# Two-layer attention hybrid on one core: three recurrence chains with two chunk lengths, a step-paired layout, zero products, and the last 128 queries on their own

## The chip, the cores and the metric

One core of a Trainium2 chip runs the whole program. The metric is the device time of one execution in microseconds (us), as the median of several runs. Before the change: 2581.43 us, median of 3 runs (2579.11 to 2581.67).

## What is computed

The input x is 4 batches of 128 channels by 4096 positions, fp32. Layer 0 normalizes by groups of channels and adds full attention over the positions (queries and keys of 64 channels, softmax over 4096 keys). Layer 1 normalizes over channels (written `_ln_t`) and adds causal attention with 128 channels. Then comes the part that this change is mostly about:

```python
def _L1_ffn_ref(x, W, V, gamma, beta):
    Wx = jnp.einsum('bti,hi->bth', x, W)
    flat = Wx.reshape(B * T, H)
    mean = jnp.mean(flat, axis=0); var = jnp.var(flat, axis=0)
    Wx = ((flat - mean) * jax.lax.rsqrt(var + BN_EPS) * gamma + beta).reshape(B, T, H)
    def step(yt, wx_t):
        yt = jax.nn.sigmoid(wx_t + yt @ V.T)
        return (yt, yt)
    _, ys = jax.lax.scan(step, jnp.zeros((B, H)), jnp.swapaxes(Wx, 0, 1))
    return jnp.swapaxes(ys, 0, 1)
...
x = x + _L0_conv_ref(_gn(x), ...)
t = _to_tokens(x)
t = t + _L1_attn_ref(_ln_t(t), ...)
t = t + _L1_ffn_ref(_ln_t(t), ...)
```

The mean and variance run over all 4 x 4096 tokens, so no step of the recurrence can start before the last query of the last batch is through the attention.

## The kernel before

**Attention.** For each batch, layer 0 and then layer 1 are cut into tiles of 512 queries (QT). A tile walks over its keys in units of two blocks of 128 keys. `score` issues the products of a unit (L892 for layer 1, L899 for layer 0) into a PSUM pair and ScalarE's exp (L901, L905); on the diagonal GpSimd zeroes the upper triangle of a block (L908). `product`, one unit behind, adds the exponentials into a running sum on VectorE (L933, `total`) and multiplies them with the values (L936, `av`). After a tile, `finish` folds `total` over the keys' partitions (L766 to L781: an add, a transpose, a reduction, small copies, a reciprocal, a transpose back), scales (L783, `o`), projects (L795, `po`) and adds the residual (L798). `ffn` then takes the layer norm of that tile (L689 transposes, L693 and L695 statistics, L561 and L562 the reciprocal root, the last on GpSimd), spreads it (L705 to L709), multiplies by W (L748, `pw`), scales (L752), copies the result into the recurrence's store WX (L753) and takes batch statistics (L758). These pieces are generators: `step` advances them once per unit, so they run between the units of the next tile. `following` and LAST = 3 give an order to the tiles of the last batch's layer 1: tile 3 comes last, in two halves of 256 queries.

**Recurrence.** The 4096 steps of a batch are cut into 128 chunks of 32 that run side by side as columns. Each chunk but the first starts from 0.5 and warms up over the last 12 steps of the chunk before it (WARM), so there are 12 + 32 = 44 steps. Two chains run in turn: batches 0 and 1, and batches 2 and 3, each with 2 x 128 = 256 columns. A step of a chain (`advance`) is one fp32 product with V (L1024, two TensorE instructions) onto a PSUM tile that already holds the scaled input, and one sigmoid (L1025) that writes into WX in place. `seed` puts the scaled input of four steps into PSUM (L1014, VectorE); a product with zeros first (L1008, `nil`) marks a new PSUM tile as written. WX is laid out as [batch, step in chunk, chunk], so one step's 256 columns are contiguous. Before the chains, the batch statistics are folded (L985), and the gain takes a reciprocal root on GpSimd (L561, L562, L988).

**Result.** X holds t in order of position, so step l of all chunks is every 32nd element. `residual` adds WX to it (L1029): for batches 0, 1 and most of 2 on GpSimd during the chains, for the rest of 2 and all of 3 on VectorE after them. Then all four batches are stored in halves of 1 MB from SP's and ScalarE's queues (L1053). Meanwhile the chunks' warm-up values are compared with the true ones (L1061 to L1074, `ok`, `wrong`); every engine loads the verdict (L1082) and branches (L1083) past a general version of the kernel, which isn't run here. Order within an engine is that of the built program: a scheduling layer may move an instruction ahead of others that it doesn't depend on.

Of the kernel before, what the change touches and what calls it, by code (L numbers as in the profile page):

```python
# [464 lines left out]
CHUNK = 32  # L465
# [5 lines left out]
BL = 4  # L471
LAST = 3
# [3 lines left out]
def fast_kernel(  # L476
# [14 lines left out]
    NP = N // (2 * P)  # L491
    NC = N // CHUNK
    G = 4
    assert C == P and 2 * CQ == P and N % QT == 0 and NC == P
# [60 lines left out]

    WXp = [wxpool.tile([P, 2, CHUNK, NC], F32, name=f"WX{g}") for g in range(B // 2)]
    WX = [WXp[b // 2][:, b % 2] for b in range(B)]
# [6 lines left out]
    with ExitStack() as actx:  # L564
# [71 lines left out]
        def keys0(b, c):  # L636

            if c == 0:
                K0[b] = kv.tile([P, N], F32R, tag="K0", name=f"K0_{b}")
                QR[b] = kv.tile([P, N // 2], F32, tag="QR", name=f"QR_{b}")  # L640
                V0[b] = WX[B - 1].rearrange("p l s -> p (l s)").rearrange("p (n c) -> p n c", c=C)
# [95 lines left out]
        def ffn(b, c, off, w):  # L737
            name = f"f_{b}_{c}_{off}"
            cols = ds(c * QT + off, w)
            src = X2[b][:, cols]  # L740
            if b < len(kept):
                nc.sync.dma_start(out=kept[b][:, cols], in_=src)
            yield
            _, _, rstd = deviations(src, 1e-5, name)
            yield
            rb = spread(rstd, name)
            pw = misc(f"pw_{name}")[:, :w]
            nc.tensor.matmul(pw, lhsT=FWc, rhs=src, start=True, stop=True)  # L748
            if off == 0:
                wt[b, c] = tmp.tile([P, QT], F32, tag="w", name=f"w_{name}")  # L750
            part = wt[b, c][:, ds(off, w)]
            nc.vector.tensor_tensor(part, pw, rb, ALU.mult)  # L752
            nc.scalar.copy(  # L753
                WX[b][:, :, ds((c * QT + off) // CHUNK, w // CHUNK)].rearrange("p l s -> p s l"),
                part.rearrange("p (s l) -> p s l", l=CHUNK),
            )
            if off + w == QT:
                nc.vector.bn_stats(stats_f[:, b * NQ + c, :], wt.pop((b, c)))  # L758
            yield

        def finish(b, layer, c, off, w, av, total):

            name = f"{layer}_{b}_{c}_{off}"
            k = w // 32
            t = tmp.tile([P, QT], F32, tag="a", name=f"t_{name}")[:, :w]
# [19 lines left out]
            )  # L785
            cols = ds(c * QT + off, w)
# [5 lines left out]
            yield  # L792
            yield
            po = misc(f"po_{name}")[:, :w]
# [8 lines left out]
        units, following = [], {}  # L803
        for b in range(B):
            for layer in range(2):
                order = list(range(NQ))
                if (b, layer) == (B - 1, 1):
                    order.append(order.pop(LAST))
                following.update({(b, layer, c): d for c, d in zip(order, order[1:])})
                for c in order:  # L810
                    halves = [(0, QT // 2), (QT // 2, QT // 2)] if (b, layer, c) == (B - 1, 1, order[-1]) else [(0, QT)]
                    for off, w in halves:
                        n = (c * QT + off + w) // (2 * P) if layer else NP
                        units += [(b, layer, c, off, w, u, n) for u in range(n)]
# [22 lines left out]
        def begin_tile(b, layer, c):  # L837
# [19 lines left out]
            else:  # L857
# [5 lines left out]
                if (b, 1, c) in following:  # L863
                    d = following[b, 1, c]
                    todo.insert(0, ("q1", b, d))
                    made["q1", b, d] = after(b, d)
# [9 lines left out]
        def score(i):  # L876
# [11 lines left out]
            first = [max(j0 + h, 0) * P if layer else 0 for h in range(2)]  # L888
            for h in range(2):
                lhsT = (X if layer else K0)[b][:, ts(2 * u + h, P)]  # L890
                if layer:
                    nc.tensor.matmul(  # L892
                        ps[:, h, first[h] : w], lhsT=lhsT, rhs=q[:, off + first[h] : off + w],
                        start=True, stop=True,
                    )
                    continue

                for k in range(2):
                    nc.tensor.matmul(ps[:, h, :], lhsT=lhsT, rhs=q[:, k, :], start=k == 0, stop=k == 1)  # L899
            if not layer:  # L900
                nc.scalar.activation(s, ps, AF.Exp, bias=shift)  # L901
            for h in range(2 if layer else 0):
# [3 lines left out]
                if j0 >= 0:  # L906
# [7 lines left out]
        def product(i):  # L914
# [7 lines left out]
            both = first[0] == first[1]  # L922
            if u == 0:
                if not both:
                    nc.vector.memset(total[:, 1, : first[1]], 0.0)
                for h in (slice(0, 2),) if both else range(2):
                    f = 0 if both else first[h]
                    nc.vector.tensor_copy(total[:, h, f:w], s[:, h, f:w])
            else:
                for h in (slice(0, 2),) if both else range(2):  # L930
                    f = 0 if both else first[h]
# [3 lines left out]
            for h in range(2):  # L935
                nc.tensor.matmul(  # L936
                    av[:, first[h] : w], lhsT=V[:, 2 * u + h, :], rhs=s[:, h, first[h] : w],
                    start=u == 0 and h == 0, stop=u == n - 1 and h == 1,
# [6 lines left out]
            if u == n - 1:  # L945
# [28 lines left out]
    with ExitStack() as fctx:  # L974
# [20 lines left out]
        nil = small.tile([P, QT], F32R, name="nil")  # L995
        nc.vector.memset(nil.bitcast(F32), 0.0)
        first = [small.tile([P, 2, NC], F32, name=f"first{g}") for g in range(B // 2)]
        for g in range(B // 2):
            nc.vector.memset(first[g], 0.5)
        steps = list(range(CHUNK - WARM, CHUNK)) + list(range(CHUNK))  # L1000
        nk = len(steps) // BL
        where = {}

        def seed(g, k):
            ps = where[g, k] = ps_y.tile([P, BL, 2, NC], F32, tag=f"y{g}", name=f"py{g}_{k}")
            if k < 2:
                for j in range(0, BL, 2):
                    nc.tensor.matmul(  # L1008
                        ps[:, j : j + 2].rearrange("p j h s -> p (j h s)"), lhsT=nil[:, :P], rhs=nil,
                        start=True, stop=True,  # L1010
                    )
            j0, lo = steps[k * BL], int(k * BL < WARM)
            for js in [slice(j, j + 1) for j in range(BL)] if k == 0 else [slice(0, BL)]:
                nc.vector.tensor_scalar(  # L1014
                    ps[:, js, :, lo:].rearrange("p j h s -> p h j s"),
                    WXp[g][:, :, j0 + js.start : j0 + js.stop, : NC - lo], gain, None, ALU.mult,
                )

        def advance(g, k, j):
            n, lo = k * BL + j, int(k * BL < WARM)  # L1020
            dst = first[g][:, :, 1:] if lo else WXp[g][:, :, steps[n], :]
            y = dst if lo else first[g] if n == WARM else WXp[g][:, :, steps[n] - 1, :]
            ps = where[g, k][:, j, :, lo:]
            nc.tensor.matmul(ps, lhsT=FV, rhs=y, start=False, stop=True, skip_group_check=True)  # L1024
            nc.scalar.activation(dst, ps, AF.Sigmoid, bias=bias)  # L1025

        def residual(eng, b, ls, cols=slice(0, NC)):
            xj = X[b].rearrange("p (s l) -> p l s", l=CHUNK)[:, ls, cols]
            eng.tensor_tensor(xj, xj, WX[b][:, ls, cols], ALU.add)  # L1029

        for k in range(2):
            for g in range(B // 2):
                seed(g, k)
        for k in range(nk):
            for j in range(BL):
                for g in range(B // 2):
                    advance(g, k, j)
            if k == WARM // BL - 1:
                for g in range(B // 2):
                    nc.vector.memset(first[g][:, :, 0:1], 0.0)  # L1040
            for g in range(B // 2 if k + 2 < nk else 0):
                seed(g, k + 2)
            if k * BL >= WARM:
                ls = slice(steps[k * BL], steps[k * BL] + BL)
                for b in range(3 if k < nk - 2 else 2):
                    residual(nc.gpsimd, b, ls)
        residual(nc.vector, 2, slice(CHUNK - 2 * BL, CHUNK))
        for h in range(2):
            residual(nc.vector, 3, slice(0, CHUNK), ts(h, NC // 2))
        for b in range(B):  # L1050
            for h in range(2):
                cols = ts(h, N // 2)
                (nc.scalar if h else nc.sync).dma_start(out=out[b, :, cols], in_=X[b][:, cols])  # L1053


        ones = small.tile([P, P], F32, name="ones")
        nc.vector.memset(ones, 1.0)
        ok = small.tile([P, B, NC], F32, name="ok")
        nc.vector.memset(ok, 0.0)
        for b in range(B):  # L1060
            nc.vector.tensor_tensor(  # L1061
                ok[:, b, 1:], first[b // 2][:, b % 2, 1:], WX[b][:, CHUNK - 1, : NC - 1], ALU.subtract
# [4 lines left out]
        nc.vector.tensor_reduce(good[:, 0:1], ok.rearrange("p b s -> p (b s)"), AX.X, ALU.min)  # L1067
# [3 lines left out]
        pf = ps_y.tile([P, BL, 2, NC], F32, tag="y0", name="pflag")[:, 0, 0, :]  # L1071
# [52 lines left out]
```

## Time and profile before

| | us |
|---|---|
| median of 3 runs | 2581.43 |
| the profiled execution, whole | 2581.84 |
| its span, first to last instruction | 2580.0 |
| TensorE busy in the span | 2510.6 (97%) |
| VectorE busy | 1761.0 (68%) |
| ScalarE busy | 1140.3 (44%) |
| GpSimd busy | 227.7 (9%) |
| end of the last attention product | 2476.2 |
| first product of the recurrence | 2495.74 |
| end of the last sigmoid | 2553.70 |
| first issue of a store, last one | 2554.80, 2565.95 |

All times in the text are counted from the span's start. A group of instructions stands as: line, engine, operation, out<-in with shapes, count, then busy time and mean duration of one in ns, then the idle time of its engine just before and what ended it. In a table of stretches (windows) each engine has its busy time and the count, and PEclk is the share of full TensorE clock that was granted. A matmul's duration contains some 0.16 us in which the next one already runs, so products are counted here by the distance between starts.

### The profile page before, as it was taken

To read this page: it belongs to the slowest core of one execution; us is meant where nothing else is said; L and a number is where in the kernel's file an instruction comes from. 1 tells how busy PE (TensorE), PEld (TensorE's weight loads), DVE (VectorE), ACT (ScalarE), POOL (GpSimd) and SP (SyncE) were. 2 spreads that over 40 slices of the span, in tenths; PEclk is the share of its full clock that TensorE was granted. 3 is DMA by queue.
4 is the path that set the end of the run, shared out by engine and by line. 5 is a ranking of instruction groups with operands and counts; after the bars stand their busy time and mean duration, and the time that the engine had idled before them with its cause. 6 is when DMAs were issued, how large, how long until landed. Compare 5 with 4: busy or idle time off the path is not lost.

```text
span 2580.0 us, 21857 instructions
## 1 busy us (share of the span) xinstructions
PE 2510.6 (97%) x7436; PEld 1350.5 (52%) x7436; DVE 1761.0 (68%) x3513; ACT 1140.3 (44%) x1386; POOL 227.7 (9%) x297
## 2 busy tenths in 40 slices
PE   7999999999999999999999999999999999999975
PEld 4555554444555555444555555444455555544552
DVE  6776667567867677666777666755786766776564
ACT  4444444444444444444444444444444444344444
POOL 2010001101000100010100010110100000000005
PEclk9999999999999999999999999999999999999988
DMA  2000000000100000000100000000010000000013
GB/s 73 1 0 1 0 1 13 9 4 5 37 1 1 1 0 5 13 5 9 37 1 0 1 0 1 13 9 4 5 37 1 1 1 1 1 0 1 1 66 132
DMA packets 11944, 31.30 MB, mean 12 GB/s; under 512 B 2096, under 2 KB 2864, under 8 KB 10032
## 3 DMA queue, kind: packets, MB, share of 16 engines
q1 hardware_dynamic: 8928, 24.12, 2.6%
q10 hardware_dynamic: 2896, 5.71, 0.6%
q8 instruction: 60, 0.98, 0.2%
q14 instruction: 60, 0.49, 0.1%
HBM read 15.14 MB, written 14.68 MB: 12 GB/s over the span
## 4 chain that ended last, share of the span: by engine, by line
PE 88%; DVE 8%; issue 2%; POOL 1%; ACT 1%; POOLq 0%; DVEq 0%; ACTq 0%
PE av L936 47%; PE ps L899 17%; PE ps L892 16%; PE py L1024 2%; DVE total L933 2%; PE po L795 1%; PE pv L666 1%; PE pk L650 1%; PE pq L731 1%; PE pw_f L748 1%; POOL rstd_f L562 1%; PE pt L689 1%; DVE lst_f L693 0%; DVE t L766 0%; ACT s L901 0%
## 5 line engine op out<-in xcount | busy, mean ns | idle before, releaser
L933 DVE TENSOR_TENSOR total<-total,s 128x1024 f32<-128x1024 f32 (+4 forms) x802 | 881.2, 1102 | 569.0 <-ACT s L901 325.6
L936 PE MATMUL av<-s,WX 128*128 128x512 f32 x2048 | 964.9, 593 | 2.3 <-ACT s L901 2.3
L901 ACT ACTIVATE s<-ps,shift 128x1024 f32<-128x1024 f32 x512 | 569.3, 1114 | 754.7 <-PE ps L899 736.2
L899 PE MATMUL ps<-q,K 128*128 128x512 f32 x2048 | 758.4, 492 | 1.2 <-DVE K L661 1.2
L905 ACT ACTIVATE s<-ps,zero,R 128x512 f32<-128x512 f32 (+1 forms) x590 | 399.9, 729 | 461.4 <-PE ps L892 460.8
L936 PEld LDWEIGHTS av<-s,WX 128*128 128x128 f32 x2048 | 382.7, 189 | 301.2 <-issue 257.7
L899 PEld LDWEIGHTS ps<-q,K 128*128 128x128 f32 x2048 | 386.3, 189 | 289.8 <-issue 235.0
L936 PE MATMUL av<-s,V 128*128 128x512 f32 (+3 forms) x1180 | 502.2, 548 | 0.5 <-ACT s L905 0.5
L892 PE MATMUL ps<-q,X 128*128 128x512 f32 (+3 forms) x1180 | 501.8, 547 | 0.0
L892 PEld LDWEIGHTS ps<-q,X 128*128 128x128 f32 x1180 | 222.0, 190 | 237.6 <-issue 227.2
L936 PEld LDWEIGHTS av<-s,V 128*128 128x128 f32 x1180 | 218.7, 190 | 223.7 <-issue 203.3
L562 POOL TENSOR_TENSOR rstd<-rstd,mhalf 128x4 f32<-128x4 f32 x32 | 32.7, 1023 | 964.6 <-DVE rstd L561 964.6
L908 POOL TENSOR_SCALAR_AFFINE_SELECT s<-s 128x128 f32<-128x128 f32 x128 | 46.4, 367 | 536.1 <-ACT s L905 535.6
L647 POOL TENSOR_SCALAR X<-X,B0v 128x512 f32<-128x512 f32 x32 | 67.6, 2115 | 251.1 <-DVE xg L645 249.6
L753 ACT COPY WX<-w_f 128x512 f32<-128x512 f32 (+1 forms) x33 | 35.3, 1069 | 89.2 <-DVE w_f L752 89.2
L562 POOL TENSOR_TENSOR rstd_f<-rstd_f,mhalf 128x4 f32<-128x4 f32 (+1 forms) x33 | 36.1, 1093 | 400.3 <-DVE rstd_f L561 400.3
L722 DVE TENSOR_SCALAR V<-pt,lmv,rstd 128x128 f32<-128x128 f32 x128 | 43.8, 404 | 35.8 <-POOL rstd L562 35.8
L795 PE MATMUL po<-o,W1v 128*128 128x512 f32 (+1 forms) x66 | 34.8, 609 | 16.1 <-DVE o L783 16.1
L680 DVE TENSOR_TENSOR q<-QR,qh 64x512 fp32r<-64x512 f32 x64 | 43.9, 685 | 6.3 <-PE ps L899 5.7
L766 DVE TENSOR_TENSOR t<-total 128x512 f32<-128x512 f32 (+1 forms) x65 | 44.4, 683 | 4.4 <-PE pfw L606 2.5
L662 ACT CAST K<-kh 64x512 fp32r<-64x512 f32 x32 | 19.7, 617 | 62.3 <-DVE kh L660 62.3
L768 DVE STREAM_TRANSPOSE tt<-t 128x512 f32<-128x512 f32 (+1 forms) x65 | 45.6, 702 | 1.9
(123 smaller groups left out, 1332.8 us busy)
## 6 DMA issues: line engine op xcount, KB each, us to landing
X<-in_x SPq DMA_DIRECT2D x28, 256.0 KB, 5.6
kept<-X SPq DMA_DIRECT2D x24, 256.0 KB, 2.0
Y<-kept SPq DMA_DIRECT2D x6, 1024.0 KB, 7.7
out<-Y SPq DMA_DIRECT2D x3, 1024.0 KB, 9.7
out<-Y ACTq DMA_DIRECT2D x3, 1024.0 KB, 10.2
X<-in_x ACTq DMA_DIRECT2D x4, 256.0 KB, 5.6
out<-X SPq DMA_DIRECT2D x1, 1024.0 KB, 15.7
out<-X ACTq DMA_DIRECT2D x1, 1024.0 KB, 12.2
```

Source lines behind the costliest of these rows:

```text
L562: nc.gpsimd.tensor_tensor(dst, dst, mhalf[:, :n], ALU.pow)
L647: nc.gpsimd.tensor_scalar(xt, xt, B0v, None, ALU.add)
L768: nc.vector.transpose(tt, t)
L795: nc.tensor.matmul(po, lhsT=W1v, rhs=o, start=True, stop=True)
L892: nc.tensor.matmul(ps[:, h, first[h] : w], lhsT=lhsT, rhs=q[:, off + first[h] : off + w], start=True, stop=True,)
L899: nc.tensor.matmul(ps[:, h, :], lhsT=lhsT, rhs=q[:, k, :], start=k == 0, stop=k == 1)
L901: nc.scalar.activation(s, ps, AF.Exp, bias=shift)
L905: nc.scalar.activation(part, ps[:, h, first[h] : w], AF.Exp, scale=scale, bias=zero)
L908: nc.gpsimd.affine_select(out=edge, in_=edge, pattern=[[1, P]], base=0, channel_multiplier=-1, compare_op=ALU.is_ge, fill=0.0,)
L933: nc.vector.tensor_tensor(t, t, s[:, h, f:w], ALU.add)
L936: nc.tensor.matmul(av[:, first[h] : w], lhsT=V[:, 2 * u + h, :], rhs=s[:, h, first[h] : w], start=u == 0 and h == 0, stop=u == n - 1 and h ...
L1024: nc.tensor.matmul(ps, lhsT=FV, rhs=y, start=False, stop=True, skip_group_check=True)
```

## The change

1. **The last tile.** The order of tiles is natural again; tile 7 of the last batch comes last, cut into 384 and 128 queries. Key blocks may now be odd in number. For the last 128, `finish` sums over keys with TensorE (a product with ones, `pz`) and takes a reciprocal of 128 columns; `ffn` brings 1/std to the columns with one product (`prow`) in place of `spread`. For the 384, the projection waits 5 units in place of 2.
2. **Zero products.** `idle` multiplies a zero tile by itself (fp32r, 512 columns): 4 after `pz`, 7 ahead of `prow`, 5 after it, and one for every step of the recurrence from the 29th on.
3. **Three chains.** Batch 0 and batch 1 each become a chain with chunks of 16 (256 chunks, 28 steps); batches 2 and 3 stay together with chunks of 32 (44 steps), and from the 29th step on they advance as two halves of 128 columns. A seed covers two steps.
4. **Layout.** WX becomes [step pair, chunk, step of the pair]: two steps of a chunk are neighbours, and the 256 columns of one step lie 8 bytes apart.
5. **Residuals and stores.** All residuals go to VectorE, during the chains: batch 0 while three chains run, batches 1, 2 and 3 after. Batches 0 and 1 are stored from SP's queue during the recurrence, 2 and 3 at the end.
6. Small tiles (zeros, ones, 0.5, ok) are now set by GpSimd.

```diff
-CHUNK = 32
+CHUNK = (16, 16, 32, 32)
-BL = 4
-LAST = 3
+LAST = 384
...
+    WX = [wxpool.tile([P, CHUNK[b] // 2, NC[b], 2], F32, name=f"WX{b}") for b in range(2)]
+    WXp = wxpool.tile([P, 2, CHUNK[2] // 2, NC[2], 2], F32, name="WXp")
+    def idle(ps, n):
+        for _ in range(n):
+            nc.tensor.matmul(ps, lhsT=nil, rhs=nil.unsqueeze(1).to_broadcast([P, QT // P, P]), start=True, stop=True)
...
+            if w == QT - LAST:
+                nc.tensor.matmul(pw, lhsT=FWc, rhs=src, start=True, stop=True)
+                raw = tmp.tile([P, QT], F32, tag="a", name=f"raw_{name}")[:, :w]
+                nc.scalar.copy(raw, pw)
+                prow = misc(f"prow_{name}")
+                idle(prow, 7)
+                nc.tensor.matmul(prow[:, :w], lhsT=rstd.to_broadcast([P, P]), rhs=ident, start=True, stop=True)
+                nc.vector.tensor_tensor(part, raw, prow[:, :w], ALU.mult)
+                idle(misc(f"idle_{name}"), 5)
...
+            if w == QT - LAST:
+                pz = misc(f"pz_{name}")
+                for h in range(2):
+                    nc.tensor.matmul(pz[:, :w], lhsT=ones, rhs=total[:, h, :w], start=h == 0, stop=h == 1)
+                idle(misc(f"idle_{name}"), 4)
+                nc.vector.reciprocal(rb, pz[:, :w])
+                nc.vector.scalar_tensor_tensor(o, rb, GUARD, av[:, :w], ALU.mult, ALU.mult)
+                yield from project(b, layer, c, off, w, o, 0)
+                return
...
+        chains = ((0,), (1,), (2, 3))
+        def seed(g, k):
...
+            nc.vector.tensor_scalar(
+                ps[:, :, :, lo:].rearrange("p t h s -> p h t s"),
+                src[:, :, : NC[b] - lo, :].rearrange("p h s t -> p h t s"), gain, None, ALU.mult,
+            )
+        def advance(g, n):
...
+            parts = [slice(h, h + 1) for h in range(2)] if n >= last else [slice(0, m)]
+            for hs in parts:
...
+                nc.tensor.matmul(ps, lhsT=FV, rhs=y, start=False, stop=True, skip_group_check=True)
+                nc.scalar.activation(dst, ps, AF.Sigmoid, bias=bias)
+        def residual(b, l, n):
+            xj = X[b].rearrange("p (s l t) -> p l s t", l=CHUNK[b] // 2, t=2)[:, l // 2 : (l + n) // 2]
+            nc.vector.tensor_tensor(xj, xj, WX[b][:, l // 2 : (l + n) // 2], ALU.add)
...
+        late = [(1, l, 4) for l in range(0, CHUNK[1], 4)]
+        late += [(b, l, 8) for l in range(0, CHUNK[2] - 8, 8) for b in (2, 3)]
+        late += [(b, l, 4) for l in (CHUNK[2] - 8, CHUNK[2] - 4) for b in (2, 3)]
+        for n in range(len(steps[2])):
+            for g in range(3):
+                advance(g, n)
+            if n >= last:
+                idle(rest, 1)
...
+            if n % 2:
+                for g in range(3):
+                    seed(g, n // 2 + 2)
+            if WARM < n < last and (n + 1) % 4 == 0:
+                residual(0, n - WARM - 3, 4)
+                if n == last - 1:
+                    store(0)
+            elif n >= last and late and WARM + late[0][1] + late[0][2] <= n:
+                b, l, k = late.pop(0)
+                residual(b, l, k)
+                if b == 1 and l + k == CHUNK[1]:
+                    store(1)
+        for b, l, k in late:
+            residual(b, l, k)
+            if l + k == CHUNK[b]:
+                store(b)
```

## The prediction

> **What bounds the kernel now.** I read the page's slices and chain first.
>
> ```profile
> PE   7999999999999999999999999999999999999975
> PEclk9999999999999999999999999999999999999988
> PE 88%; DVE 8%; issue 2%; POOL 1%; ACT 1%; POOLq 0%; DVEq 0%; ACTq 0%
> ```
>
> TensorE fills the span but for its last twentieth. The built program has the same order of instructions in both kernels up to the last batch's second layer, so only the end counts. A table of stretches over it:
>
> ```profile
> core 0: us, PE busy (x) PEld busy (x) DVE busy (x) ACT busy (x) POOL busy (x), PEclk, DMA share, GB/s
> 2456.00:2476.20 20.20, 17.60 (x85) 14.73 (x83) 14.80 (x52) 10.93 (x20) 2.70 (x6) 1.00 0.00 1
> 2476.20:2495.70 19.50, 6.51 (x14) 3.80 (x14) 14.85 (x59) 1.54 (x4) 1.94 (x3) 0.62 0.55 216
> 2495.70:2501.50 5.80, 5.76 (x13) 3.61 (x14) 2.79 (x4) 2.41 (x6) 0.00 (x0) 0.50 0.00 0
> 2501.50:2553.70 52.20, 51.70 (x164) 24.20 (x163) 22.87 (x20) 39.30 (x83) 31.69 (x21) 1.00 0.00 0
> 2553.70:2566.00 12.30, 0.00 (x0) 0.00 (x0) 12.30 (x6) 0.01 (x1) 2.64 (x2) 0.60 0.85 353
> 2566.00:2580.00 14.00, 0.58 (x2) 0.50 (x2) 2.56 (x8) 0.00 (x0) 0.00 (x0) 0.50 0.73 295
> ```
>
> Four stages: attention with a hole, 19.5 us in which VectorE folds the last queries, the recurrence (5.8 us at half clock), and 26.3 us of residuals and stores. Within them, the timeline and the chain of waits (start, us, what):
>
> ```profile
> 2468.35 0.70 PE L795 MATMUL po<-o,W1v 128*128 128x256 f32 x2 [2.58 <-DVE o L783]
> 2554.80 3.82 SPq L1053 DMA_DIRECT2D out<-Y  x3
> 2565.95 0.34 ACTq L1053 DMA_DIRECT2D out<-X  x1
> ```
> ```profile
> 2469.91 0.86 PE ps L892 x4
> ...
> 2495.74 56.80 PE py L1024 x174
> ...
> 2558.26 7.65 DVE X L1029 x2
> ```
>
> Four 256-column instructions take 0.86 us, so 0.215 each. The chain ends with the verdict at 2569.4; what ends the span is the stores. 8.39 MB leave between 2554.8 and 2577.65 (last packet) at 400 GB/s, then come 2.3 us. Last, the groups by shape:
>
> ```profile
> L933 DVE TENSOR_TENSOR total<-total,s 128x1024 f32<-128x1024 f32 x671 | 818.0, 1219 | 522.1 <-ACT s L901 325.6 <-ACT s L905 190.9
> L777 DVE RECIPROCAL z<-z 32x16 f32<-32x16 f32 x63 | 15.2, 240 | 2.0
> L1029 DVE TENSOR_TENSOR X<-X,WX 128x2048 f32<-128x2048 f32 x2 | 7.8, 3979 | 0.0
> L777 DVE RECIPROCAL z<-z 32x8 f32<-32x8 f32 x2 | 0.3, 156 | 0.0
> ```
>
> An add of contiguous columns costs 1.19 ns per element, one whose X lies 128 bytes apart 1.94.
>
> **Attention's end.** The products are the same in number of columns. Gone: the hole of 2.6 us before `po`. Added: 128 more columns of `po`, transposes and `pw` run inside (0.5 us). The 16 units of 128 queries have eight instructions of 0.107 us each, 0.86 us a unit; the trace has 128-column ones start 0.109 us apart in the diagonal blocks, so weight loads don't bind. Their exps (0.45 us, the second 0.35 later) fit in. But VectorE must do the 384's fold (about 4.4 us) beside four adds of 0.46 us, while exp waits for a buffer that the adds free: 1.5 us lost, between 0 and 2.6, since the old hole was of this kind. Sum -0.3; last add to `total` at 2476.2 (before: 2475.9).
>
> **From the last add to the first recurrent product.** New path: `pz` 0.75 (load 0.11, four times 0.109, drain and semaphore 0.2); reciprocal of 128 columns: no row has it; 8 more elements cost 84 ns in L777, so 0.156+120 x 10.5 ns = 1.4 us (0.3 at one element per cycle, 1.8 at the steepest pair); `o` 0.3; `po` 0.55; X 0.32; transpose 0.43; statistics 0.3+0.18+0.18; GpSimd's root 0.65 (549 ns for one column); `prow` 0.95, since seven zero products (0.215 each) start only when the transposes' buffer is read and end 0.55 us after the root; scaling 0.33; L758 0.72; L985 1.05; L561 0.18, GpSimd 0.65, L988 0.18; first seed of 512 elements 0.8 (254 take 0.48, 1016 1.27). Sum 10.1 us, where before 19.5 passed. Weights broadcast from one column (`prow`) have no row: not below an ordinary load of 0.19, above by perhaps 0.5; I take the former. GpSimd's memsets (1 to 2 us by their sizes) end before its root is wanted.
>
> Does the clock hold? The Trainium skill ("TensorE: Matmul & The Clock Gate", "Why this matters for your kernels") warns of idle gaps over about 3 us. Here a shorter hole did it, at a batch's border: a gap of 2.3 us before 654.3, then one window at half clock:
>
> ```profile
> 651.50:654.90 3.40, 1.29 (x5) 0.57 (x5) 3.33 (x17) 1.11 (x1) 0.00 (x0) 1.00 0.00 0
> 654.90:658.30 3.40, 3.40 (x6) 1.34 (x5) 2.73 (x9) 0.00 (x0) 1.01 (x1) 0.51 0.22 80
> ```
>
> By the rule the new path, whose gaps stay under 1.8 us, is safe without zero products. By the row, a window only about a third busy loses the clock; the thinnest new one (around `po`) has 1.56 us of work in 3.41 with the zero products (half of `pz`, four zero products, `po`, transpose, `pw`, two and a half of the seven), 46%, and the hole at 2468 with about 47% kept it. So I take full clock; else +3 us (1.7 as before in the recurrence, 1.5 for zero products at half rate).
>
> **Recurrence.** Before: 1.26 us per step, the latency of one chain (load and product 0.70, sigmoid 0.474, semaphores). Three chains: TensorE 3 x 2 x 0.215 = 1.29; ScalarE 3 x 0.37 to 0.47 (a following exp starts 0.1 before the duration is over) = 1.1 to 1.4; latency 1.26. I take 1.35: 28 steps, 37.8 us. The last chain starts 1.3 us after the first, behind two more seeds of 0.65 (back to back).
> VectorE per two steps: three seeds, 1.95 of 2.7 us; batch 0's residuals (1.2 each, one per four steps) bring it to 5.1 of 5.4. That assumes the contiguous rate. The skill ("Advanced Engine Details and Errata", "Memory Cachelines") says SBUF has lines of 16 bytes and that two hits per line suffice for full rate: in the new layout every access has two, in the old residual one. By the rule a residual of 1024 elements costs 1.2 us, by L1029's row 2.0. I take the rule, as the row has one hit; pairs lie between.
> Halves of 128 columns: latency 1.26 less 0.215 (half the product) less 0.11 (exps of 256 and 128: 562, 450 ns) = 0.94; 16 steps, 15.1. Zero products: the built order has not one per step but blocks of three between the first four half products; the second of those steps takes 1.74 in place of 0.94, the next 0.15 more: +1.0. On VectorE, residuals (ten of 1.2, two of 0.65) stand between the seeds, and one that waits for its own sigmoid holds up the seed behind it, for which TensorE waits. By the built order, counted from the last chain's start: batch 0's last residual can begin at 37.6; it and one more end at 40.05, the seed of pair 15 at 40.7, two residuals and the seed of pair 16 at 43.75, which was wanted at 42.7 (1.05 late); likewise pair 17 is 1.1 late and pair 19, behind two `ok` comparisons and a residual, 0.8: +3.0 (0 if they fit). Sum 37.8+15.1+1.0+3.0 = 56.9, against 57.96 before.
> ScalarE's copies into WX (1.10 us each) may get shorter; ScalarE waits hundreds of us for TensorE, so I count nothing; without that cover 31 copies would weigh some 10 us.
>
> **End.** Last residuals end 1.3 us after the last sigmoid, where before 12.2 passed. Batches 0 and 1 (4.2 MB, 10 us) are out by then; their issues stand on SP, behind nothing that waits. Batches 2 and 3 take 4.19 MB / 400 GB/s = 10.5, about 1.0 to start, 2.3 after: 15.1. The other path: verdict 4 us after the last residual, 1.3 to load it, TensorE's branch 7.3 (its instruction fetch shares the DMA engines), 1.8: 1.3+14.4 = 15.7. I take 15.5, against 26.3.
>
> **Sum.** 2476.2+10.1+1.3+56.9+15.5 = 2560.0 span; the profiled execution lies 1.84 above its span: 2561.8, rounded to 2562, against its 2581.84, which is 0.4 above the median of 2581.43. That small difference I leave in the range. Forecast 2562, its own range 2555 to 2568.
>
> **Rivals.**
> Pairs not free (20%): residuals at 1.94 ns per element. Eleven of 1024 from the 24th step on cost 0.8 more each while VectorE already sets the pace: +9, 2571. For it: the only strided VectorE row. Against: those rows ran beside saturated DMA, with one hit per line.
> Three chains collide (8%): sigmoids 0.5 apart give 1.5 per step, +4.2; with the clock lost, +3: 2566 to 2569.
> No queueing (7%): 1.29 per step (-1.7), no late seed (-3.0), no loss in the 128-query units (-1.5), fast reciprocal (-1): 2554.8.
> Slower (6%): 8-byte strides halve VectorE's rate in the seeds too. 50 seeds of 512 elements at 1.2 us and 16 residual equivalents at 2.0 are 92 us on VectorE; the recurrence follows it, +35, 2597. It is slower from about 1.85 ns per element, over all 42,000, on; against it, the rule and two hits per line.
> That the change doesn't do what it says: early stores gain nothing if the branch ends the span. Then still 15.7, as above.
>
> **Numbers.** Forecast 59%, rivals 20, 8, 7, 6. The range 2553 to 2573 leaves out the slower case and the tails of the others. About 0.2% (5 us) is what a measurement tells from no change: faster 0.92, same 0.02, slower 0.06.
>
> **What would show it.** First recurrent product near 2486, PEclk 1.00 from 2476 to the last sigmoid; 1.35 us per three-chain step; residuals (L1069) near 1.2 us per 1024; some 19 us for the last 16 steps; last sigmoid near 2544.5; no store of batches 0 and 1 left when it ends. A recurrence over 66 us, or residuals of 2 us, prove the forecast wrong.

## The result, and the profile after

The changed kernel takes 2571.64 us, median of 7 runs (2569.48 to 2572.47), against 2581.43 (2579.11 to 2581.93) before: a ratio of 0.9963, 95% interval 0.9952 to 0.9975. It gained 9.8 us where 19.4 were forecast (2581.43 to 2562). The profiled execution has a span of 2570.4 and took 2572.15.

The page's slices of TensorE and its clock, and the chain that ended last:

```profile
PE   7999999999999999999999999999999999999996
PEclk9999999999999999999999999999999999999997
PE 90%; DVE 7%; issue 1%; ACT 1%; POOL 1%; DMA 0%; SPq 0%; POOLq 0%; DVEq 0%; ACTq 0%
```

TensorE's share of the last slice is larger than before, and the clock granted there is lower. Stretches of the last 114 us, cut at the last add to `total`, the first recurrent product, the 29th step of the third chain, the moment at which the clock halves, and the last sigmoid (each engine's busy time with its count, then granted clock, DMA share, GB/s):

```profile
core 0: us, PE busy (x) PEld busy (x) DVE busy (x) ACT busy (x) POOL busy (x), PEclk, DMA share, GB/s
2456.00:2475.30 19.30, 17.26 (x137) 15.96 (x136) 14.05 (x48) 13.98 (x34) 1.14 (x2) 1.00 0.01 2
2475.30:2485.30 10.00, 7.88 (x35) 5.42 (x34) 5.47 (x19) 1.28 (x4) 2.59 (x6) 1.00 0.87 346
2485.30:2524.20 38.90, 38.88 (x173) 29.33 (x173) 36.86 (x51) 37.30 (x84) 0.00 (x0) 1.00 0.05 20
2524.20:2534.10 9.90, 7.27 (x37) 5.03 (x36) 8.43 (x9) 4.06 (x12) 0.00 (x0) 1.00 0.99 410
2534.10:2555.20 21.10, 13.70 (x39) 9.24 (x38) 8.20 (x12) 7.57 (x21) 0.00 (x0) 0.50 0.02 6
2555.20:2570.40 15.20, 0.59 (x2) 0.50 (x2) 3.82 (x8) 0.01 (x1) 0.00 (x0) 0.50 0.69 281
```

Against the two traces, three terms explain the difference. The first recurrent product comes 10.4 us earlier (2495.74 to 2485.32). From there to the last sigmoid takes 69.9 us in place of 58.0, a loss of 11.9. What follows the last sigmoid takes 15.2 in place of 26.3, 11.1 won. The sum is -9.6, as the spans say. Stores of batches 0 and 1 fill the fourth row (410 GB/s) and are out before the last sigmoid, as forecast. The loss sits in rows four and five: 31.0 us for 16 steps. TensorE, ScalarE and VectorE are each idle for much of it, and after a third of it the clock drops to half.

The timeline there (start, us, engine, line, with what it had waited for), first at full clock, then at half:

```profile
2528.34 0.50 PE L1064 MATMUL py<-WXp,FV 128*128 128x128 f32 x2 [0.26 <-ACT WXp L1065]
2528.88 0.38 ACT L1065 ACTIVATE WXp<-py,fbias 128x128 f32<-128x128 f32 x1 [0.59 <-PE py L1064]
2529.31 0.49 PE L1064 MATMUL py<-WXp,FV 128*128 128x128 f32 x2 [0.47 <-ACT WXp L1065]
2529.84 0.38 ACT L1065 ACTIVATE WXp<-py,fbias 128x128 f32<-128x128 f32 x1 [0.58 <-PE py L1064]
2530.27 0.72 PE L1064 MATMUL py<-WXp,FV 128*128 128x128 f32 x4 [0.47 <-ACT WXp L1065]
...
2531.50 0.49 PE L1064 MATMUL py<-WXp,FV 128*128 128x128 f32 x2 [0.50 <-ACT WXp L1065]
...
2538.86 0.80 PE L1064 MATMUL py<-WXp,FV 128*128 128x128 f32 x2 [0.47 <-ACT WXp L1065]
2539.69 0.38 ACT L1065 ACTIVATE WXp<-py,fbias 128x128 f32<-128x128 f32 x1 [0.89 <-PE py L1064]
2540.12 0.80 PE L1064 MATMUL py<-WXp,FV 128*128 128x128 f32 x2 [0.47 <-ACT WXp L1065]
```

(An x2 row of TensorE is one product of a half, x4 two of them.) Two halves that ran side by side would have a product of one under the sigmoid of the other. Here product, sigmoid, product, sigmoid follow one another: TensorE always waits for the sigmoid just issued, ScalarE for the product just issued. Only once in two steps do two halves go together (the x4 row), where the product belongs to the next PSUM tile. Three such hops (0.97, 0.96, 1.23) make 3.16 us for two steps; at half clock the same pattern takes 4.21 (2538.86 to 2543.07), in hops of 1.26, 1.26 and 1.69.

### The profile page after: what moved, and what is told of

Its sections match the earlier page's. It is cut to its first block, busy times and chain, and to the rows that moved or that the text cites. A ratio compares the mean times of both kernels' runs of the same rounds, so it can differ in the third digit from the quotient of the medians.

```text
span 2570.4 us, 22293 instructions
## 1 busy us (share of the span) xinstructions
PE 2514.2 (98%) x7596; PEld 1370.0 (53%) x7596; DVE 1771.7 (69%) x3534; ACT 1140.2 (44%) x1432; POOL 194.5 (8%) x281
## 4 chain that ended last, share of the span: by engine, by line
PE 90%; DVE 7%; issue 1%; ACT 1%; POOL 1%; DMA 0%; SPq 0%; POOLq 0%; DVEq 0%; ACTq 0%
PE av L966 48%; PE ps L928 17%; PE ps L921 16%; PE py L1064 2%; DVE total L963 2%; PE po L829 1%; PE pv L675 1%; PE pq L740 1%; PE pw_f L770 1%; PE pk L659 1%; PE pt L698 1%; PE pt_f L698 0%; ACT s L930 0%; POOL rstd_f L571 0%; ACT WXp L1065 0%
## 5 line engine op out<-in xcount | busy, mean ns | idle before, releaser
L963 DVE TENSOR_TENSOR total<-total,s 128x1024 f32<-128x1024 f32 (+5 forms) x810 | 881.7, 1091 | 563.1 <-ACT s L930 325.2
L966 PE MATMUL av<-s,WXp 128*128 128x512 f32 x2048 | 964.1, 593 | 0.9 <-ACT s L930 0.9
L934 ACT ACTIVATE s<-ps,zero,R 128x512 f32<-128x512 f32 (+3 forms) x607 | 404.5, 717 | 462.6 <-PE ps L921 461.1
L966 PEld LDWEIGHTS av<-s,WXp 128*128 128x128 f32 x2048 | 382.4, 189 | 299.3 <-issue 257.4
L571 POOL TENSOR_TENSOR rstd_f<-rstd_f,mhalf 128x4 f32<-128x4 f32 (+2 forms) x33 | 35.8, 1085 | 408.6 <-DVE rstd_f L570 408.6
L797 DVE TENSOR_TENSOR t<-total 128x512 f32<-128x512 f32 x64 | 44.1, 689 | 4.4 <-PE pfw L615 2.5
L799 DVE STREAM_TRANSPOSE tt<-t 128x512 f32<-128x512 f32 x64 | 45.3, 708 | 1.9
L814 DVE SCALAR_TENSOR_TENSOR o<-rb,av 128x512 f32<-128x512 f32 x64 | 43.6, 681 | 4.1
L812 DVE STREAM_TRANSPOSE rb<-z 128x512 f32<-128x512 f32 x64 | 45.0, 703 | 1.1
```

Source lines behind the costliest of these rows:

```text
L571: nc.gpsimd.tensor_tensor(dst, dst, mhalf[:, :n], ALU.pow)
L799: nc.vector.transpose(tt, t)
L812: nc.vector.transpose(rb, z[:, :k].unsqueeze(2).to_broadcast([P, k, 32]))
L934: nc.scalar.activation(part, ps[:, h, first[h] : w], AF.Exp, scale=scale, bias=zero)
L963: nc.vector.tensor_tensor(t, t, s[:, h, f:w], ALU.add)
L966: nc.tensor.matmul(av[:, first[h] : w], lhsT=V[:, 2 * u + h, :], rhs=s[:, h, first[h] : w], start=u == 0 and h == 0, stop=2 * u + h == n - 1,)
```

## The experiments

**Theory A**: both halves of a step write one PSUM tile. A product that stands behind a sigmoid of that tile in the program waits for it, so the halves go one after the other. In addition the clock is lost, because the 16 zero products meant to keep it (L566) had been moved ahead by the scheduling layer, the last of them into the 31st step. **Rival B**: the clock alone. **Rival C**: VectorE's late seeds. Ratios below are to the kernel before, with 95% intervals; "16 steps" is from the first half product to the end of the last sigmoid in the profiled execution (31.0 after the change).

### Whole steps (e1_whole)

```diff
-parts = [slice(h, h + 1) for h in range(2)] if n >= last else [slice(0, m)]
+parts = [slice(0, m)]
```

> The last 16 steps are taken whole: one product and one sigmoid of 256 columns per step instead of two halves of 128. Theory A (the halves run one after the other because both write one PSUM tile, three hops of 0.96 us per two steps at full clock, and the clock halves at 2534 because little is left for TensorE): one chain costs 1.26 us per step at full clock, as before the change, and about 1.85 at half clock; with the zero products still in front of the first steps the last sigmoid ends near 2549 (2545 if the clock holds) in place of 2555.2, and the time is 2561 to 2566 us. Rival B (the clock alone; halves overlap as soon as it is full): whole steps are no shorter than halves, 2571 us or more.

Measured 2566.55 us, 0.9945 (0.9930 to 0.9960). The 16 steps take 25.2 us although the clock is lost here too, at 2533.8. The chain at half clock:

```profile
2537.03 1.23 PE py L1064 x2
2538.29 0.50 ACT WXp L1065
2538.83 1.24 PE py L1064 x2
```

One undivided step takes 1.80 us at half clock, less than the 2.1 of two halves in a row. B, which had halves no slower than whole steps, falls: on a shared tile the split itself costs 5 us.

### A tile for each half, and zero products that can't be moved (e2_banks, e3_fed, e4_banks_fed)

```diff
+if m > 1 and 2 * k >= last:      # e2, e4: in seed
+    for h in range(2):
+        where[g, k, h] = ps_y.tile([P, 2, 1, NC[0]], F32, tag=f"y{h}", ...)
+        # seed of this half alone
...
-idle(rest, 1)                    # e3, e4
+nc.tensor.matmul(rest[:, :P], lhsT=nil, rhs=y, ...)   # behind each half product; e4: every second step
```

> Each half of the last 16 steps gets PSUM tiles of its own (those of the two short chains, which are free by then), so no tile is shared by two halves; seeds become two of 256 elements; zero products stay where they are. Theory A (shared tile): halves overlap, 0.96 us per step at full clock and 1.26 at half; VectorE's own work in that stage, about 19 us, then sets the pace; last sigmoid near 2542 to 2545, the time 2558 to 2562 us. Rival B (the clock alone): it is lost as before, the two steps still take 4.2 us, 2570 to 2573. Rival C (VectorE's late seeds set the pace): more seed instructions, 2571 or more.

> The 16 hoisted zero products are replaced by zero products of 128 columns that read the same y as each half product, so that they can't be moved ahead of their step; halves still share a tile. Theory A: the clock stays full, but the halves still go one after the other: 3.15 us per two steps plus 0.25 for a zero product in the way, 25 to 27 us for 16 steps, last sigmoid near 2550, the time 2565 to 2568 us. Rival B (the clock alone): with the clock full the halves overlap, 16 to 19 us, the time 2557 to 2560. If neither the clock nor the tile matters: 2571.

> Both: tiles of its own for each half, and in place of the 16 hoisted zero products two of 128 columns in every second step that read that step's y. Theory A with the clock: 0.96 us per step at full clock, so 15.4 us unless VectorE's 19 us of seeds and residuals set the pace; last sigmoid 2539 to 2543, the time 2555 to 2559 us, at or below the kernel with tiles of its own alone. If the clock costs nothing once the halves overlap: equal to it. If VectorE's seeds are the limit (C): no better than 2565.

Measured: e2 2558.99 us, 0.9918 (0.9905 to 0.9932); e3 2566.34, 0.9946 (0.9931 to 0.9961); e4 2560.03, 0.9920 (0.9906 to 0.9933). The 16 steps as one stretch, in this order, e2, e3, e4:

```profile
2524.55:2542.10 17.55, 14.75 (x75) 11.35 (x74) 15.82 (x24) 10.80 (x32) 0.00 (x0) 0.89 0.58 239
```
```profile
2524.20:2550.00 25.80, 21.45 (x128) 16.53 (x128) 16.48 (x21) 11.20 (x32) 0.00 (x0) 1.00 0.40 163
```
```profile
2524.90:2541.70 16.80, 15.39 (x96) 12.44 (x96) 15.89 (x24) 12.03 (x32) 0.00 (x0) 1.00 0.61 251
```

The clock column of e3 is 1.00, and still the steps take 25.8 us: with a shared tile a full clock gives 5.2 of the 31.0 back, no more. B falls for the second time. With a tile for each half, 17.6 us are enough although nothing was done for the clock, and C falls, since e2 has more seeds on VectorE than the changed kernel; in that kernel TensorE waited for a seed only once behind the first product, 0.2 us. With own tiles the clock is nearly a side matter: e2 loses it only at 2538.2, for its last 3.9 us, and e4, which keeps it, needs 0.75 us less for the 16 steps and yet ends no sooner. (Its end behind the last sigmoid took 17.4 us in place of e2's 16.1; why is not shown.) In e4 the DVE column (15.89 of 16.80) names one candidate for what comes next, the PE column (15.39) another. A, with both its parts, stands.

### Both products ahead of both sigmoids (e5_order)

```diff
+    sig.append((dst, ps))        # products of both halves first
...
+for dst, ps in sig:
+    nc.scalar.activation(dst, ps, AF.Sigmoid, bias=bias)
```

> Halves share one PSUM tile again (and so one bank), but both products of a step come ahead of both sigmoids in the program, with one zero product of 128 columns per step that reads that step's y, in place of the 16. Theory A1 (the wait that kept the halves apart comes from the program's order on a shared tile: a product that follows a sigmoid of that tile waits for it): within a step the second product no longer waits; a step is two products, two sigmoids and the hand-over, about 1.15 to 1.25 us, 18 to 20 us for 16 steps, last sigmoid 2542 to 2544, the time 2559 to 2562 us. Theory A2 (the chip itself can't write a bank while ScalarE reads it): products and sigmoids go one after the other as before, 1.57 us or more per step, the time 2565 to 2568 us, as with the shared tile at full clock.

Measured 2562.81 us, 0.9931 (0.9916 to 0.9946), a little above A1's range; the 16 steps take 21.5 us at full clock, where 18 to 20 were expected. The 16 steps, and the timeline within them:

```profile
2523.60:2545.10 21.50, 15.40 (x96) 12.25 (x96) 15.64 (x20) 10.11 (x32) 0.00 (x0) 1.00 0.47 195
```
```profile
2533.08 0.72 PE L1065 MATMUL py<-WXp,FV 128*128 128x128 f32 x4 [0.50 <-ACT WXp L1070]
2533.84 0.63 ACT L1070 ACTIVATE WXp<-py,fbias 128x128 f32<-128x128 f32 x2 [0.81 <-PE py L1065]
```

A half product alone ended 0.5 us after its start in the rows above; here the first half's sigmoid begins 0.76 after the start, behind both products: on a shared tile a sigmoid also waits for every product ahead of it in the program. That is why a step took 1.34 (21.5 / 16) and not 1.2.

The built programs carry these waits as counts of an engine's finished work. In the changed kernel the second half's product of the 31st step waits until ScalarE's count is 1403, which its sibling's sigmoid makes it; its own y is ready at 1402. In e5_order the first sigmoid of a step waits for the product of the second half too. In e2_banks each product waits for its own y and its seed, and each sigmoid for its own product. So the order of the program decides who waits, as A1 has it. No product wrote while ScalarE read that tile, so what the chip would do without the wait (A2) is not shown. The Trainium skill ("PSUM — Partial Sum Buffer", "PSUM bank collisions raise a hardware error") says that two engines must not access one bank on the same partitions at once, not even in different columns; a tile of this pool is 512 fp32 columns, by that page a whole bank, so the wait is then needed and not only cautious. No run here shows a collision, and none was tried.

### Zero products in the tail (e6_tail_bare)

```diff
-idle(misc(f"idle_{name}"), 4)
...
-idle(prow, 7)
...
-idle(misc(f"idle_{name}"), 5)
```

> The 16 zero products between the last add and the first recurrent product (four behind the sums, seven ahead of the broadcast of the root, five behind it) are left out; nothing else. By the skill's rule (gaps under about 3 us cost nothing): the clock stays full and the broadcast starts 0.45 us earlier, first recurrent product near 2484.9 in place of 2485.3, the time 2571 us. By the row of the batch border (a window a third busy costs a window of 3.41 us at half clock): the window around the reciprocal or the one of the root falls below a third, TensorE runs at half clock for 3.4 us or more in there, first recurrent product or the first steps 1.5 to 3 us later, the time 2573 to 2575.

Measured 2573.33 us, 0.9972 (0.9962 to 0.9982), inside the row's range; its interval overlaps that of the changed kernel, so the trace decides. Three stretches of this kernel:

```profile
2474.60:2478.00 3.40, 1.41 (x9) 0.83 (x7) 2.02 (x8) 0.48 (x3) 1.24 (x4) 1.00 0.76 251
2478.00:2484.90 6.90, 5.42 (x13) 4.16 (x14) 4.41 (x12) 0.36 (x2) 1.09 (x2) 0.51 1.01 426
2484.90:2523.80 38.90, 38.86 (x175) 29.33 (x173) 36.18 (x49) 37.31 (x84) 0.00 (x0) 1.00 0.03 12
```

Without them the clock halves at 2478.0 and stays so for 6.9 us, although TensorE's longest gap in the 3.4 us before is 1.37 us. The row of the batch border was the better guide than the rule on gaps, but a third was too low a mark: TensorE was busy for 41% of the 3.4 us before the loss. The price is small: from last add to first recurrent product 10.8 us in place of 10.0, as the path there consists mostly of VectorE's and GpSimd's work.

### Stores moved in the program, then held by data (e7_stores_end, e10_stores_held)

```diff
-store(0)   # and store(1), in the loop
+store(0)   # behind the last residual, with the others            (e7)
...
+nc.vector.scalar_tensor_tensor(xh, yl, 0.0, xh, ALU.mult, ALU.add)  # e10: needs the last step
+store(b)
```

> The stores of batches 0 and 1 are issued after the last residual, with those of 2 and 3; nothing else. If the stores set the end: 8.39 MB at 410 GB/s are 20.5 us, with 1.0 to start and 2.3 behind them 23.8 us in place of 15.2 after the last residual or so, the time 2580 to 2582 us. Rival (the branch behind the verdict ends the span in any case, early stores gain little): 2571 to 2575 us.

> Stores of batches 0 and 1 held back, now by data: two columns of each batch have zero times an output of the last step added to them (0.3 us of VectorE), so that its stores can't start before the last sigmoid; moving the issue in the program alone had left the transfers at 2524 to 2536 and the time at 2571.7. If the stores set the end: 8.39 MB at 410 GB/s, 23.8 us in place of 15.2 behind the last sigmoid, the time 2580 to 2582 us. If the branch behind the verdict ends the span in any case: it shares the DMA engines with 8.39 MB of stores, 2571 to 2576 us.

Measured: e7 2571.74 us, 0.9967 (0.9955 to 0.9978); e10 2581.74, 1.0003 (0.9995 to 1.0012). The first taught nothing on stores. The scheduling layer put the issues back behind the residuals they depend on (SP's built order is that of the changed kernel), and the transfers stood at 2524 to 2536 as before. Its number looks like a hit of the rival and is none. Held by data, the stores cost 10.1 us more than in the changed kernel. Three stretches of e10:

```profile
2523.30:2535.00 11.70, 8.54 (x39) 5.88 (x38) 9.72 (x12) 4.68 (x14) 0.00 (x0) 0.90 0.00 0
2535.00:2554.70 19.70, 12.85 (x36) 8.73 (x36) 6.91 (x10) 7.09 (x19) 0.00 (x0) 0.50 0.00 0
2554.70:2579.40 24.70, 0.58 (x2) 0.50 (x2) 3.96 (x10) 0.02 (x1) 0.00 (x0) 0.50 0.84 343
```

No byte of a store moves before the last sigmoid, and the end takes 24.7 us in place of 15.2. The verdict is ready at 2559.6, in the changed kernel at 2559.9, so it isn't what came later. Without the early stores, this kernel is no faster than the one before.

### The old tail (e11_tail_old)

```diff
-LAST = 384
+LAST = 256
...
-if w == QT - LAST:     # twice
+if w == 0:             # the new path is never taken
```

> The last 512 queries again as 256 and 256, folded and scaled on VectorE as all other tiles are (transposes, 32-column sums, reciprocals), without the 16 zero products there; recurrence and stores as after the change. If the way from the last add to the first recurrent product is worth what the two traces show (20.3 us before, 10.0 after), the first recurrent product comes near 2495.6 and the time is 2580 to 2582 us. If the tail hid behind something else (the Y loads, which run at that time): 2572 to 2576 us.

Measured 2577.80 us, 0.9988 (0.9982 to 0.9995): between the two expectations, 6.2 us more than the changed kernel. From last add to first recurrent product:

```profile
2471.57:2487.16 15.59, 7.63 (x20) 5.01 (x20) 11.20 (x41) 0.96 (x3) 2.74 (x6) 0.56 0.68 269
```

That is 15.6 us in place of 10.0, at a clock of 0.56. But its last add ends at 2471.57, where the kernels with the 128 queries apart have it between 2473.9 and 2476.0 (2475.3 in the changed one): attention itself ends later with them. Part of what the short path saves behind the last add is paid ahead of it. It isn't the old tail in full, either: the order of tiles stays natural, and the last add comes 4.3 us before that of the kernel before (2475.87), whose way from there was 19.9 us and not 20.3. Its profiled execution was the fastest of its 20 runs (3.6 us above the changed kernel's), so how the 6.2 divide isn't settled.

### What bounds the halves once they overlap (e8_best, e9_whole_fed, e12_less)

```diff
+residual(1, n - WARM - 3, 4, nc.gpsimd)     # e8, with e4; and batches 0, 1 of the verdict on GpSimd
...
+nc.tensor.matmul(rest[:, : 2 * P]..., lhsT=nil, rhs=y, ...)   # e9: whole steps, zero product reads y
...
-late = [(1, l, 4) for l in range(0, CHUNK[1], 4)]            # e12, with e4
```

> Tiles of its own for each half, two zero products in every second step that read its y, and two pieces of VectorE's work moved to GpSimd: batch 1's residuals (during the 28 steps) and batches 0's and 1's part of the verdict. If VectorE's work was what set the pace once the halves overlap: 16 steps at 0.96 to 1.0 us, last sigmoid 2539.5 to 2540.5 in place of 2541.6, and the verdict 1.0 us shorter, the time 2555 to 2557 us. If GpSimd slows VectorE in the three-chain steps: the third chain comes later by some us, 2559 to 2562. If neither matters: 2559 to 2560.

> The last 16 steps whole (256 columns), with one zero product of 256 columns per step that reads the step's y in place of the 16 hoisted ones. The clock then stays full: 1.26 to 1.30 us per step as before the change, 20 to 21 us, last sigmoid near 2543.5 to 2544.5, the time 2560 to 2563 us, 4 to 6 below whole steps with the clock lost (2566.6). If the clock matters less than that: 2565 or more. Against the halves with tiles of their own (2559 to 2560): no more than 4 us apart, since VectorE's work of some 19 us lies under both.

> Tiles of its own for each half and the zero products that read y; batch 1's four residuals (4.9 us of VectorE) are left out, so that batch 1's output lacks its last addition. If VectorE's seeds and residuals set the pace of the last 16 steps once the halves overlap: 16 steps at 0.96 to 1.0 us, last sigmoid 2538 to 2539.5 in place of 2541.2, the time 2556 to 2558 us. If TensorE, the sigmoids or the clock set the pace: 2560 us as with them.

Measured: e8 2559.00 us, 0.9918 (0.9905 to 0.9932); e9 2562.33, 0.9925 (0.9909 to 0.9942); e12 2556.54, 0.9906 (0.9890 to 0.9923). The 16 steps of e12:

```profile
2522.95:2538.75 15.80, 15.34 (x96) 12.44 (x96) 12.75 (x22) 11.97 (x32) 0.00 (x0) 1.00 0.32 134
```

That is 0.99 us per step, close to the hop of one half (0.96). TensorE is busy throughout, its zero products among that, and VectorE no longer is; which of the hop and TensorE's own work sets this pace isn't told apart. VectorE's pace was worth 1.0 us (16.8 to 15.8). The rest of the 3.5 us to e4 lies outside this stretch: in the profiled executions, whose spans differ by 4.9, e12's steps begin 2.0 us earlier and its end is 1.9 shorter (15.45 to 17.4). Neither follows from the edit, and the cause isn't shown.

e9 is as expected, 20.8 us, 1.30 per step. Whole steps at full clock are some 3 us behind halves with tiles of their own.

e8 missed its 2555 to 2557 us and gained nothing over e2. Rows of its timeline, VectorE's and GpSimd's residuals and the product that follows, and a stretch:

```profile
2522.57 2.38 POOL L1080 TENSOR_TENSOR Y<-Y,WX 128x1024 f32<-128x1024 f32 x1
2522.70 3.33 DVE L1080 TENSOR_TENSOR Y<-Y,WX 128x1024 f32<-128x1024 f32 x1
...
2528.26 1.91 PE L1073 MATMUL ph<-WXp,FV 128*128 128x128 f32 x6 [1.35 <-DVE ph L1044]
```
```profile
2528.00:2532.00 4.00, 3.74 (x16) 3.44 (x16) 3.37 (x7) 1.61 (x5) 2.12 (x2) 0.57 1.03 426
```

An add that VectorE does in 1.21 us alone takes up to 3.33 beside GpSimd's (the first two rows), so the work moved away is paid back. The Trainium skill ("SBUF — State Buffer", "SBUF: two separate sides") says that the two share ports under a lock held for a whole instruction, and the rows agree: VectorE's add ends at 2526.03, 1.08 us after GpSimd's (2524.95), as if it had started only then. Two others that begin under a GpSimd add (2518.49, 2525.95) also end 1.08 or 1.09 us after it. Where VectorE's add starts first, by 0.3 us, it takes 1.22, and GpSimd's is the slow one (3.2 for 2.4). The seeds queued behind the slow adds come late, and e8's 16 steps take 18.6 us. One such seed stops TensorE for 1.35 us (the third row), and right after it the clock is at half from 2528.45 to 2531.6, although this kernel's zero products read y: they stop when their step stops.

The fastest kernel that computes everything is e2 with 2558.99 us (e8 at 2559.00 and e4 at 2560.03 can't be told from it): 22 us below the kernel before, 12.7 below the changed one, and below the forecast of 2562.

## Why the prediction was right and wrong

**Attention's end and the first recurrent product: right, the first in part by luck.** Last add 2475.3 for 2476.2, then 10.0 us for 10.1. The sums hold slips: the terms of attention's end (-2.6, 0.5, 1.5) give -0.6 and not -0.3, which from 2475.9 is the measured 2475.3, while 2476.2 was the end of the last product; those of the path add up to 9.9, and the old path from the last add was 19.9, not 19.5. Kernels with the same attention have the last add anywhere between 2473.9 and 2476.0, so agreement within 1 us there proves little. The reciprocal of 128 columns, which no row had shown, took 0.96 us for 1.4. The broadcast starts 0.66 us after the root is done, in e6 0.05, so the seven zero products cost 0.6 for 0.55. The clock held there, and e6 shows that the zero products held it.

**The three-chain steps: right.** 38.9 us from the first product to the 29th step of the third chain, for 1.3 + 37.8. TensorE is busy for 38.88 of them. The rival of colliding chains did not occur.

**Pairs: right.** The groups after, where 1.2 and not 1.94 ns per element were at stake:

```profile
L1069 DVE TENSOR_TENSOR Y<-Y,WX 128x1024 f32<-128x1024 f32 x8 | 9.6, 1216 | 0.0
...
L1065 ACT ACTIVATE WX<-py,fbias 128x256 f32<-128x256 f32 x32 | 15.1, 492 | 0.0
```

1.19 ns per element, the contiguous rate. The sigmoid over columns 8 bytes apart takes 492 ns, against 474 for contiguous columns before. Both the rival of costly pairs and the slower case fall.

**"Halves of 128 columns: ... 0.94; 16 steps, 15.1": the step that failed.** It took the latency of one half as the time of a step and so supposed that the other half fits beside it. The sum had 15.1 + 1.0 + 3.0 = 19.1 us; the trace has 31.0, and the difference of 11.9 is more than the whole error of the span (2570.4 for 2560.0; the other terms were together 1.5 us better). What the sum lacked is the wait for the sibling's sigmoid on the shared tile: two steps take three hops, 3.16 us at full clock, and not two (1.9). By e3, 25.8 of the 31.0 remain at full clock; by e2 and e4, 17.6 and 16.8 remain with a tile for each half. So sharing costs some 9 us at full clock, and the lost clock some 5 on top. The latency itself was right: a hop of product and sigmoid measured 0.96 for 0.94, and e12's 16 steps took 15.8 us. The built order held the answer: the count that the second half's product waits for is that of the sibling's sigmoid, not of its own y. The rule on PSUM banks quoted with e5_order spoke against the sum too, and was overlooked.

**"So I take full clock" and "PEclk 1.00 from 2476 to the last sigmoid": failed as well.** It was weighed for the tail only, where it held. The mark that was read from the batch border, "only about a third busy", was too low: TensorE was busy for 1.98 of the 3.41 us before the loss at 2534.1, 58%. That the 16 zero products had moved into the first steps was seen and priced at +1.0 for the place they take, but not for the clock they then no longer keep. From 2534.1 on, TensorE at half speed made a hop 1.26 us in place of 0.96.

**Late seeds, +3.0: not there, for the wrong reason.** With the halves in a row VectorE waits for ScalarE. Once they overlap, its pace costs 1.0 us (e4 against e12).

**The end: right.** 15.2 us for 15.5, and e10's 24.7 show that the stores set it: moving half of them forward is worth 10 us. In both kernels the last store lands some 1.8 us before the end (2578.15 and 2568.57). Of the other path the traces show only the whole, 10.6 us from verdict to end before and 10.5 after; its split into load, branch and rest stands in no trace. The old stores' rate was also overstated: 8.39 MB from 2554.8 to 2577.65 are 367 GB/s, and 400 hold only for the stretch between start and last packets. "A recurrence over 66 us" was named as the proof against the forecast; it took 69.9.

## What to carry to other kernels

Two pieces of work are independent only if they share no tile: before counting an overlap, look in the built order for what each instruction waits for, and give each piece a PSUM tile of its own. Zero products that are to stay in their step must read something of it, but then they stop with it, too (e8). A store that is to wait must depend on data; its place in the program did not hold it. Price a stage by the chain of one piece only after the trace or the order has shown that the next piece starts inside it.

## What the runs showed of the hardware

- **The clock is lost without long gaps.** In the changed kernel TensorE was busy 1.98 of the 3.41 us before the loss at 2534.1, in e6 1.41 of 3.40, with no gap above 1.37 us. In e5_order 2.25 of 3.40 (2530.0 to 2533.4) kept it. Before the losses in e1, e2 and e8 it was 1.65, 2.03 and 2.04 of 3.41. But the changed kernel also kept it over 1.59 of 3.40 at 2471.0 to 2474.4, so the busy share of a stretch chosen by hand doesn't tell; which stretches decide was not found out.
- **GpSimd and VectorE slow each other.** The add that starts second pays: on VectorE 3.33 us in place of 1.21, ending 1.08 us after GpSimd's; on GpSimd 3.2 us in place of 2.4. All are from e8.
- **A reciprocal costs by column**: 956 ns for 128 columns (after the change), against 156 ns for 8 and 240 for 16 (before): from 8 to 128 some 6.7 ns for each further column.
